# Loading the second half of the last expert's up weight in sixteen pieces of eight rows: a Perceiver layer with 32 experts on one core

## The chip, the cores and the metric

The kernel runs on one core of one Trainium2 chip. The metric is the device time of one execution in microseconds (us). Lower is better. Before the change three runs took 1252.88, 1253.95 and 1255.7 us; the median is 1253.95.

## The reference

The reference is one layer in float32 over 256 tokens of width 512. A cross-attention of the tokens with a context of 25088 rows comes first, then a self-attention with 16 heads, and then a feed-forward part with a shared expert and 32 routed experts. Each part is added to its input. What the change touches is the last of these, cut here to its routed experts:

```python
logits = x @ gate_w                         # 256 x 32
topk_ids = jnp.argmax(logits, axis=-1)      # one expert for each token
scores = jax.nn.sigmoid(jnp.max(logits, axis=-1))[:, None]
xs = x * scores
...                                         # tokens sorted by their expert
g = _grouped_mm(sorted_x, routed_gate_w, tokens_per_expert)   # 512 -> 1024
u = _grouped_mm(sorted_x, routed_up_w, tokens_per_expert)     # 512 -> 1024
d = _grouped_mm(jax.nn.silu(g) * u, routed_down_w, tokens_per_expert)   # 1024 -> 512
...
return (shared_out + routed_out).reshape(b, s, h)
```

Each of the 32 experts has three weights of 2 MB: gate, up and down. All are read once, 201 MB in total.

## The kernel before

**Stages.** The first 780 us are the two attentions, in which TensorE is busy nearly all the time. Then come the experts. The kernel gives each expert 32 places for tokens (`CAP`), and gathers the tokens of four experts at a time into `xg`. For each expert `e` it multiplies `xg` with the gate weight `rg_e` and with the up weight `ru_e` (line 1073; four column blocks fill the 128 rows of a PSUM bank), takes silu of the first and multiplies the two (lines 1091 and 1097), turns the result (line 1107), multiplies it with the down weight `rd_e` (line 1121), copies it out of PSUM (line 101), and adds the rows to their tokens with a product by a 0/1 matrix `selT` (line 1130).

**Weights.** Each weight lies in SBUF as a tile of 128 rows (partitions) of 4096 floats, 16 KB a row. Ten such places (`SLOTS` and `MORE_SLOTS`) take turns. The list `to_come` holds the weights in the order of their use: `rg_1`, `ru_1`, `rd_1`, `rg_2` and so on to `rd_31` (a few of the first weights are loaded apart). When a weight has been used, `done` gives its place to `feed`, which takes the next weight from the list and issues its transfer on the queue of SyncE (SP, line 135). A tiling layer assigns the semaphores and adds the waits. SP handles its instructions in order: an issue that waits holds back all that follow it.

**The last two weights.** `feed` cuts the last up weight `ru_31` into two halves of 2048 columns, and the last down weight `rd_31` into pieces of 2048, 1024 and 1024 columns, so that each product can begin before the whole weight has landed. Columns 0 to 2047 of an up weight are its first two blocks of 128 input features, columns 2048 to 4095 the last two. The product with `ru_31` at line 1073 takes the four blocks in order, with 8 of the 32 matmuls that the trace shows for each; the last 16 need the second half.

**The end.** For the last expert `last_down` (from line 1134) forms the product with `rd_31` in three parts of 256, 128 and 128 columns (line 1147), one for each piece, multiplies each with `selT_last` (line 1159), adds it to the sum `y_sb` (line 1160) and stores the part (line 1161): six stores, five on SP's queue and one on ScalarE's. `keep_clock` (line 107) issues matmuls whose results are not used, at places where TensorE would idle.

Below, `ru_31a` and `ru_31b` are the halves of `ru_31`.

Of the kernel before, what the change touches and what calls it, by code (L numbers as in the profile page):

```python
# [16 lines left out]
P = 128  # L17
# [13 lines left out]
E, I = 32, 1024  # L31
# [17 lines left out]
def perceiver_layer(  # L49
# [23 lines left out]
    nc = tc.nc  # L73
# [54 lines left out]
    def feed(slot):  # L128
        if to_come:
            name, src = to_come.pop(0)  # L130
            w = pool_of[slot].tile([P, 4096], F32, tag=f"w{slot}", name=name)
            ends = {f"ru_{E - 1}": (0, 2048, 4096), f"rd_{E - 1}": (0, 2048, 3072, 4096)}
            ends = ends.get(name, (0, 4096))
            for a, b in zip(ends, ends[1:]):
                nc.sync.dma_start(w[:, a:b], src[:, a:b])
            weights[name] = (w, slot)

    def weight(name, f):
# [2 lines left out]
    def done(name):  # L141
        feed(weights.pop(name)[1])
# [183 lines left out]
    with tc.tile_pool(name="pro", bufs=1) as pro:  # L326
# [76 lines left out]
        r = [[by[:, :, u, g, :] for g in range(2)] for u in range(2)]  # L403
# [53 lines left out]
    for slot in range(3, SLOTS):  # L457
        feed(slot)
# [246 lines left out]
    for slot in range(SLOTS, SLOTS + MORE_SLOTS):  # L705
        pool_of[slot] = late
        feed(slot)
# [675 lines left out]
```

## Time and profile before

The profile is one execution with the hardware profiler on. It took 1255.4 us, of which 1253.5 us are the span that the trace covers.

| | |
|---|---|
| median of three runs | 1253.95 us |
| profiled execution | 1255.4 us, span 1253.5 us |
| mean granted TensorE clock | 0.974 of full speed |
| TensorE (PE) busy | 1146.0 us, 91% of the span |
| VectorE (DVE), ScalarE (ACT), GpSimd (POOL) busy | 579.8, 218.9, 208.4 us |
| read from HBM | 328.82 MB, 263 GB/s over the span |

Times inside the trace count from the span's start. PE stands for TensorE's matmuls, PEld for its loads of weights into the array, SP and SPq for SyncE and its queue. "L135" is line 135 of the kernel. In a line such as "ru<-in_ro_u_dram" the tile left of the arrow is written from the one at its right, and numbers in the names of tiles are left out, so that `ru` stands for all the `ru_e`. "x2" after an issue means that two are shown in one line; its second number then reaches from the start of the first to the end of the last. In square brackets stands how long the engine was idle before, and what released it. "To landing" is the time from an issue to the arrival of its last byte.

### The profile page before, as it was taken

To read this page: it belongs to the slowest core of one execution; us is meant where nothing else is said; L and a number is where in the kernel's file an instruction comes from. 1 tells how busy PE (TensorE), PEld (TensorE's weight loads), DVE (VectorE), ACT (ScalarE), POOL (GpSimd) and SP (SyncE) were. 2 spreads that over 40 slices of the span, in tenths; PEclk is the share of its full clock that TensorE was granted. 3 is DMA by queue.
4 is the path that set the end of the run, shared out by engine and by line. 5 is a ranking of instruction groups with operands and counts; after the bars stand their busy time and mean duration, and the time that the engine had idled before them with its cause. 6 is when DMAs were issued, how large, how long until landed. Compare 5 with 4: busy or idle time off the path is not lost.

```text
span 1253.5 us, 16455 instructions
## 1 busy us (share of the span) xinstructions
PE 1146.0 (91%) x6800; PEld 836.8 (67%) x6800; DVE 579.8 (46%) x1083; ACT 218.9 (17%) x456; POOL 208.4 (17%) x172
## 2 busy tenths in 40 slices
PE   9999999999999999999999999999998777666667
PEld 7888888888888888888888766654544323222223
DVE  3577766786666866668766435421101010110001
ACT  1222221122221222212221223311000000000000
POOL 1234312333223332133322000000000000000000
PEclk9999999999999999999999999899999888898989
DMA  9654444444443444434431391699999999999997
GB/s 384 278 197 166 170 157 151 162 168 168 168 157 146 168 168 168 168 138 165 168 138 65 135 401 36 273 424 428 429 430 429 430 429 428 430 430 429 430 428 307
DMA packets 32765, 330.44 MB, mean 264 GB/s; under 512 B 3760, under 2 KB 4656, under 8 KB 5680
## 3 DMA queue, kind: packets, MB, share of 16 engines
q1 hardware_dynamic: 32400, 329.03, 65.9%
q8 instruction: 55, 0.90, 0.3%
q10 hardware_dynamic: 288, 0.33, 0.1%
q14 instruction: 22, 0.18, 0.0%
HBM read 328.82 MB, written 0.52 MB: 263 GB/s over the span
## 4 chain that ended last, share of the span: by engine, by line
PE 74%; DMA 22%; DVE 2%; issue 1%; ACT 1%; POOL 0%; DVEq 0%; ACTq 0%; SPq 0%
PE sc L483 26%; PE p L299 22%; DMA rd<-in_ro_d_dram 9%; DMA ru<-in_ro_u_dram 6%; DMA rg<-in_ro_g_dram 6%; PE rg L1073 2%; PE acc L1130 2%; PE d L1121 2%; PE ru L1073 2%; PE shg L1180 1%; PE q L753 1%; PE y L821 1%; PE vh L730 1%; PE shu L1180 1%; PE k L753 1%
## 5 line engine op out<-in xcount | busy, mean ns | idle before, releaser
L483 PE MATMUL sc<-aT,ctxT 128*128 128x256 f32 x1568 | 341.1, 379 | 0.0
L483 PEld LDWEIGHTS sc<-aT,ctxT 128*128 128x128 f32 x1568 | 297.8, 190 | 40.7 <-issue 0.2
L299 PE MATMUL p<-diffs,sums 128*128 128x256 f32 x576 | 155.9, 379 | 0.8 <-DVE diffs L285 0.8
L299 PEld LDWEIGHTS p<-diffs,sums 128*128 128x128 f32 x576 | 109.4, 190 | 16.1 <-DVE diffs L285 1.3
L487 ACT COPY st<-sc 128x512 f32<-128x512 f32 x98 | 57.4, 586 | 276.7 <-PE sc L483 276.7
L533 POOL TENSOR_TENSOR ls<-ls,st 128x512 f32<-128x512 f32 x64 | 104.2, 1628 | 3.8
L1121 PE MATMUL d<-rd,actT 128*32 128x512 f32 x496 | 74.0, 709 | 32.5 <-DMA rd<-in_ro_d_dram 25.6
L491 DVE TENSOR_TENSOR mx<-mx,st 128x512 f32<-128x512 f32 x64 | 47.0, 734 | 121.0 <-ACT st L487 120.7
L299 PE MATMUL p<-ctx,st 128*128 128x256 f32 x384 | 98.5, 379 | 0.0
L1073 PE MATMUL ru<-ru,xg 128*32 128x256 f32 x992 | 66.8, 409 | 31.5 <-DMA ru<-in_ro_u_dram 31.5
L1128 DVE TENSOR_SCALAR selT<-keys,slot_key 128x256 f32<-128x256 f32 x31 | 10.9, 354 | 164.6 <-PE acc L1130 164.6
L1097 DVE TENSOR_TENSOR act<-act,ru 128x256 f32<-128x256 f32 x32 | 13.5, 422 | 154.8 <-PE ru L1073 154.8
L299 PEld LDWEIGHTS p<-ctx,st 128*128 128x128 f32 x384 | 73.0, 190 | 9.9
L1130 PE MATMUL acc<-d,selT 128*128 128x512 f32 x124 | 64.2, 642 | 15.1 <-ACT d L101 15.1
L529 ACT ACTIVATE st<-st 128x512 f32<-128x512 f32 x98 | 59.9, 631 | 77.9 <-DVE m L511 73.2
L1073 PEld LDWEIGHTS ru<-ru,xg 128*32 128x32 f32 x992 | 31.7, 116 | 62.2 <-DMA ru<-in_ro_u_dram 39.7
L500 POOL PARTITION_ALL_REDUCE mbc<-mx x17 | 18.8, 1105 | 306.3 <-DVE mx L492 298.5
L526 DVE TENSOR_TENSOR st<-st,mbc 128x512 f32<-128x512 f32 x98 | 62.7, 685 | 0.0
L1073 PE MATMUL rg<-rg,xg 128*32 128x256 f32 x960 | 59.1, 382 | 1.7 <-DMA rg<-in_ro_g_dram 0.7
L1130 PEld LDWEIGHTS acc<-d,selT 128*128 128x128 f32 x124 | 22.1, 198 | 54.8 <-ACT d L101 38.6
L1121 PEld LDWEIGHTS d<-rd,actT 128*32 128x32 f32 x496 | 16.9, 120 | 62.0 <-issue 47.8
L299 PE MATMUL p<-ctx,sums 128*128 128x256 f32 x192 | 57.2, 380 | 0.5 <-DVE sums L280 0.5
(296 smaller groups left out, 1317.2 us busy)
## 6 DMA issues: line engine op xcount, KB each, us to landing
rd<-in_ro_d_dram SPq DMA_DIRECT2D x31, 2048.0 KB, 38.8
ru<-in_ro_u_dram SPq DMA_DIRECT2D x30, 2048.0 KB, 37.5
rg<-in_ro_g_dram SPq DMA_DIRECT2D x30, 2048.0 KB, 38.9
ctxT<-in_cxT_dram SPq DMA_DIRECT2D x49, 1024.0 KB, 4.9
ctx<-in_cx_dram SPq DMA_DIRECT2D x49, 1024.0 KB, 4.9
sh<-in_sh_gu_dram SPq DMA_DIRECT2D x2, 2048.0 KB, 18.6
w_qc_ks<-in_w_qc_ks_dram SPq DMA_DIRECT2D x2, 1024.0 KB, 12.6
w_vc_vs<-in_w_vc_vs_dram SPq DMA_DIRECT2D x2, 1024.0 KB, 15.7
```

What stands on the lines that cost most here:

```text
L299: nc.tensor.matmul(bank[n][:, ts(o, half)], left[:, i, :], right[:, h, :], start=(first and o == 0), stop=(final and (o == 1 or n == 3)),)
L483: nc.tensor.matmul(pm[:, ts(u, N)], cols[b][:, c, ts(2 * h + u, P)], aT[:, c, :], start=(c == 0), stop=(c == KC - 1),)
L487: nc.scalar.copy(st[:, i, :], pm)
L491: nc.vector.tensor_tensor(mx, mx, st[:, i, :], ALU.max)
L526: nc.vector.tensor_tensor(pair, pair, mbc.to_broadcast([P, 2, N]), ALU.subtract)
L529: nc.scalar.activation(st[:, i, :], st[:, i, :], AF.Exp, scale=xscale)
L533: nc.gpsimd.tensor_tensor(ls, ls, st[:, i, :], ALU.add)
L753: nc.tensor.matmul(pm[:, :N], w[:, c, ts(hp, P)], h1T[:, c, :], start=(c == 0), stop=(c == KC - 1),)
L1073: given["up"] = nc.tensor.matmul(pm[ts(q, CAP), : I // 4], xg[:, c, ts(j, CAP)], w[c][:, ts(q, I // 4)], start=(i == 0), stop=(i == KC - 1),)
L1121: nc.tensor.matmul(pd[ts(q, CAP), :], actT[:, k, ts(q, CAP)], wd_e[:, k, q], start=(k == 0), stop=(k == 1),)
L1130: summed = nc.tensor.matmul(accs[t], slT[:, ts(t, P)], d, start=start, stop=stop)
L1180: nc.tensor.matmul(pm[:, :N], w[:, o + c, ts(i % 4, P)], h2T[:, c, :], start=(c == 0), stop=(c == KC - 1),)
```

## The change

The second half of `ru_31` no longer comes in one transfer of 128 rows and 1024 KB. It comes in sixteen transfers of eight rows each, 64 KB a piece, issued on the same queue at the same place, one after the other. The first half and the three pieces of `rd_31` are as before; `rd_31` still follows `ru_31` on the queue.

```diff
@@ -129,10 +129,14 @@
         if to_come:
             name, src = to_come.pop(0)
             w = pool_of[slot].tile([P, 4096], F32, tag=f"w{slot}", name=name)
-            ends = {f"ru_{E - 1}": (0, 2048, 4096), f"rd_{E - 1}": (0, 2048, 3072, 4096)}
+            ends = {f"ru_{E - 1}": (0, 2048), f"rd_{E - 1}": (0, 2048, 3072, 4096)}
             ends = ends.get(name, (0, 4096))
             for a, b in zip(ends, ends[1:]):
                 nc.sync.dma_start(w[:, a:b], src[:, a:b])
+            if name == f"ru_{E - 1}":
+
+                for r in range(0, P, 8):
+                    nc.sync.dma_start(w[r : r + 8, 2048:], src[r : r + 8, 2048:])
             weights[name] = (w, slot)
 
     def weight(name, f):
```

## The prediction

> **What bounds the kernel now.** I read the page first: its slices and its chain.
>
> ```profile
> DMA  9654444444443444434431391699999999999997
> ...
> PE 74%; DMA 22%; DVE 2%; issue 1%; ACT 1%; POOL 0%; DVEq 0%; ACTq 0%; SPq 0%
> ```
>
> The last 15 of 40 slices have the DMA engines full (9) at about 430 GB/s: the stretch in which the experts' weights stream in. Then the chain of waits in order of time, its end:
>
> ```profile
> 1178.27 38.83 DMA rd<-in_ro_d_dram
> 1217.10 0.14 issue
> 1217.23 2.97 PE d L1121 x16
> ```
>
> Up to 1217 us the path is transfers laid end to end; after that TensorE's work for the last three experts runs, close behind the stream. How close, the timeline of the last microseconds tells:
>
> ```profile
> 1240.51 2.13 PE L1073 MATMUL ru<-ru,xg 128*32 128x256 f32 x32
> 1241.57 0.59 PEld L1073 LDWEIGHTS ru<-ru,xg 128*32 128x32 f32 x16 [0.47 <-DMA ru<-in_ro_u_dram]
> ...
> 1245.23 0.38 PEld L1147 LDWEIGHTS d_last<-rd,actT_last 128*32 128x32 f32 x16 [0.43 <-DMA rd<-in_ro_d_dram]
> ```
>
> The second half of ru_31 (the transfer that is changed) and the second piece of rd_31 are each waited for, by 0.47 and 0.43 us. So there is no slack behind them: a later landing is a later end, one for one. An earlier landing can give back at most 0.47 + 0.43 = 0.9 us.
>
> What decides is when SP may issue. The timeline of SP alone:
>
> ```profile
> 1168.44 0.33 SPq L135 DMA_DIRECT2D rg<-in_ro_g_dram  x1
> ...
> 1202.58 5.12 SPq L135 DMA_DIRECT2D ru<-in_ro_u_dram  x2
> 1212.27 10.07 SPq L135 DMA_DIRECT2D rd<-in_ro_d_dram  x3
> ```
>
> The two halves of ru_31 come from one loop, with nothing between them in the code, yet 5.12 us pass from the start of the first issue to the end of the second: the second starts at 1202.58 + 5.12 - 0.33 = 1207.37. The rg issued at 1168.44 needs, by its tile's view,
>
> ```profile
> DMA to landing us min/median/max: 38.9/38.9/38.9
> ```
>
> and lands at 1207.3. It is the eighth transfer before this one. The rule holds at each of the last issues: an issue waits for the landing of the transfer eight before it (38.9 us is also 8 times 2,048 KB at 431 GB/s). The first output store shows it too, in SP's waits and in the view of line 1161:
>
> ```profile
> SPq L1161 <- DMA ru<-in_ro_u_dram: 3.7, 1, 3.7
> ...
> L1161 SPq EVENT_SEMAPHORE  x5: 17/17/32, 1226.9 to 1249.2; - x5
> ```
>
> Its data are ready at 1247, but first it waits until 1226.9 for ru_30, eight transfers earlier and no input of it. So at most eight transfers are in flight, whatever their size. The last five, ru_31 in two and rd_31 in three, take from issue to landing:
>
> ```profile
> DMA to landing us min/median/max: 36.5/36.5/36.5
> ...
> DMA to landing us min/median/max: 34.2/34.2/34.2
> ...
> DMA to landing us min/median/max: 31.7/31.7/31.7
> ...
> DMA to landing us min/median/max: 28.1/28.1/28.1
> ...
> DMA to landing us min/median/max: 24.4/24.4/24.4
> ```
>
> Issued at 1202.6, 1207.4, 1212.3, 1217.1 and 1222.0, they land at 1239.1, 1241.6, 1244.0, 1245.2 and 1246.4.
>
> **The change part by part.** It removes one 1,024 KB transfer and adds sixteen of 64 KB, p0 to p15, ahead of rd_31 on SP's queue. The work of TensorE, VectorE and ScalarE is the same.
>
> *Where the sixteen are issued.* p0 takes the removed transfer's place at 1207.4. By the rule of eight p1 waits for ru_29 (1212.3), p2 rd_29 (1217.1), p3 rg_30 (1222.0), p4 ru_30 (1226.9), p5 rd_30 (1231.8), p6 rg_31 (1236.6), and p7 the first half of ru_31, at 1239.1. When that lands, only p0 to p6 stand behind it (448 KB), where now 3 MB do. These seven hide behind older transfers and cost nothing. p8 to p15 wait for p0 to p7, which land within about 2 us after 1239.1, so SP's own pace sets them.
>
> *SP's pace.* The trace has bursts of issues that wait for nothing, as at the kernel's start:
>
> ```profile
> 2.17 0.43 SPq L156 DMA_DIRECT2D w_kc_qs<-in_w_kc_qs_dram  x1
> 2.65 0.45 SPq L162 DMA_DIRECT2D bias_sb<-in_biases_dram  x1
> 3.13 0.44 SPq L329 DMA_DIRECT2D selT<-in_midT_dram  x1
> ```
>
> One per 0.48 us, and the 26 KB transfer costs no less than the 1 MB ones. Elsewhere a second issue follows after 0.37 (23.04 to 23.41) and a third after 0.54 (to 23.95). No issue of eight rows is in the trace; I take 0.45 with ends of 0.37 and 0.54, since the size does not show.
>
> *The second half of ru_31.* p15 is issued at 1239.1 + 8 x 0.45 = 1242.7. A 1,024 KB load into an idle queue takes 4.8 us (ctx at 112.9 us), of which 2.44 is data at 430 GB/s, so 2.4 is fixed; one 8 KB row on one of 16 engines at 430/16 = 27 GB/s adds 0.3. p15 lands 2.7 later (ends: 1.7, the shortest store of the page, and 3.3, the longest), at 1245.4 instead of 1241.6: +3.8 for the product.
>
> *rd_31.* It is moved from 1212.3 behind p15: 1239.1 + 9 x 0.45 = 1243.15. Its first half needs 4.8 us to 1248.0; its two quarters, 1.22 us of data each, land by 1249.2 and 1250.4, against 1246.4. Since 1239.1 + 4.8 + 2.44 is 1246.4, the delay is nine issues: 9 x 0.45 = 4.05 us (3.3 to 4.9). TensorE reaches d_last at 1244.22 + 3.8 = 1248.0, just as its first piece is there: the two delays lie beside each other, and the larger counts, **+4.1**.
>
> *New waits.* The product now waits for sixteen landings on TensorE's queue; behind it stand actT_last, d_last and part, which need it anyway. A semaphore instruction takes 17 ns in SP's row above, so seven more are 0.1 us, hidden in the idle time before p15 lands. The six output stores now wait for p11 to p15 and rd_31, landed long before their data are ready.
>
> *The clock.* TensorE idles 0.5 us before the second half now, and 4.3 with the change. What such gaps do, two of the earlier ru products show, one beside the other:
>
> ```profile
> 1197.67 3.52 PE L1073 MATMUL ru<-ru,xg 128*32 128x256 f32 x32 [2.91 <-DMA ru<-in_ro_u_dram]
> ...
> 1212.25 1.93 PE L1073 MATMUL ru<-ru,xg 128*32 128x256 f32 x32 [2.91 <-DMA ru<-in_ro_u_dram]
> ```
>
> After the same gap one ran at a granted clock of 0.50 and one at full clock. Half a product at the slow rate loses (3.52 - 1.93)/2 = 0.8. The bounds are 0 (no drop, or hidden behind rd_31) and 3 (all of 1244.2 to 1248.0 slow, at 1.8 times); since the gap is longer than those of 2.9, which already go either way, I take **+0.7**.
>
> [...]
>
> [...]
>
> **Sum.** 4.1 + 0.7 = +4.8 us. The profiled execution took 1255.4 (span 1253.5 and 1.9 around it), so it would take 1260.2. It lies 1.45 above the median of the runs; on the median the forecast is 1253.95 + 4.8 = 1258.75, about **1258.8**. 0.2% is 2.5 us, which is about what a measurement of this kernel can tell from no change.
>
> **The rivals.**
>
> *No bound of eight for such small pieces* (chance 0.10). If all sixteen were queued by 1215 and rd_31 behind them, the stream would never run dry: 1,024 KB more or less on the same engines, no change if the rows spread evenly, at most one more 2.4 us if half the engines carry it all. 1253.9 to 1256.4. Against it: the 4.84 us between issues of every size, the 64 KB-sized store among them.
>
> *Faster through the engines that are ahead* (0.02). DMA engines do not end together: at 1242 to 1246 the busy share is 0.53 and 0.41, so about half of them are done while the others still work. If the eight-row pieces fell on those, the late half would carry 64 KB less each, 2.4 us, and rd_31 would land by 1244. TensorE can use 0.9 of it: 1253.05. It decides only if p7 to p15 are queued before 1239, which the rule of eight forbids.
>
> *Each piece waits for the one before* (0.06). If the program holds the sixteen for overlapping writes of one tile, they go one by one: p1 to p15 at 2.7 + 0.1 each after 1239.3, 42 us, rd_31 after that: near 1253.95 + 40 = 1294. Nothing in the trace has two queued writes to different rows of one tile, so only the code speaks against it: the rows are disjoint.
>
> *The forecast* has 0.82. Within it, the ends 3.3 to 4.9 and 0 to 3 give 1257.2 to 1261.9.
>
> **How the numbers follow.** The range reaches down into the first rival, 1255.4, and up past the likeliest case's end by 0.6 for a p15 that lands as late as 3.3 us, 1262.5. Outside it lie the serial case (0.06), the faster one (0.02), and the part of the first rival under 1255.4 (about 0.06), with some of the forecast's tails. Faster by over 0.2%: 0.02. Within 0.2%: the first rival's 0.10 and 0.02 of the forecast with quick issues. Slower: the rest, 0.86.
>
> **What would show it.** In the changed kernel SP should issue p1 to p6 some 4.9 us apart, p7 to p15 and rd_31 in one burst of 0.4 to 0.5 each after 1239, and rd_31's pieces should take 5 to 7 us to land instead of 24 to 32. The wait for ru at line 1073 should be near 4 us at the last product, DMA share should fall below a third between 1240 and 1244, and everything before 1207 should be as it was. I am wrong if rd_31 is issued before 1239, if the burst is quicker than 0.3 or slower than 0.6 us per piece, or if each piece waits for the one before.

## The result, and the profile after

The changed kernel takes 1263.87 us (median of 6 runs, 1261.89 to 1267.97) against 1252.72 us (6 runs) before: a ratio of 1.0079, interval 1.0063 to 1.0096, or 7.9 to 12 us slower. The forecast was 1258.8 with a range to 1262.5: slower, as said, but by about twice the 4.8 us. The profiled execution took 1264.5 us, with a span of 1262.6, 9.1 more than before.

The page of the changed kernel, its slices of DMA share and its chain by engine:

```profile
DMA  9744444344444445444430573799999999999995
...
PE 73%; DMA 22%; DVE 3%; issue 1%; ACT 1%; POOL 0%; DVEq 0%; ACTq 0%; SPq 0%
```

The stream is full up to the last slice, as before; that one has 5 tenths instead of 7. The shares of the chain hardly move, and TensorE, VectorE and ScalarE do the same work in the same order, so it is the end that has to be read. The chain from ru_31a on, in order of time (start, us, what; pieces under 0.8 us are left out):

```profile
1199.88 37.97 DMA ru<-in_ro_u_dram
1237.87 3.72 DMA ru<-in_ro_u_dram
1241.61 6.03 DMA ru<-in_ro_u_dram
1247.67 1.98 PE ru L1077 x16
1251.42 2.79 PE d_last L1151 x32
1254.21 1.79 PE part L1163 x4
1257.04 0.96 DVE y_sb L1164 x4
```

The first line is ru_31a, the second p7 (issued when ru_31a lands, landed 3.7 us later), the third p15 (issued when p7 lands, landed 6.0 us later). Then TensorE takes over. rd_31 is not on the path at all. SP's timeline of the same kernel:

```profile
1199.88 0.33 SPq L135 DMA_DIRECT2D ru<-in_ro_u_dram  x1
1204.67 37.21 SPq L139 DMA_DIRECT2D ru<-in_ro_u_dram  x16
1242.36 1.79 SPq L135 DMA_DIRECT2D rd<-in_ro_d_dram  x3
```

Inside the 37.21 us the single issues of the trace start at 1204.67 (p0), 1209.52, 1214.41, 1219.31, 1224.20, 1229.10, 1234.98, 1237.87 (p7), 1238.18, 1238.52, 1238.86, 1239.19, 1239.56, 1240.20, 1240.91 and 1241.61 (p15). The rule of eight holds for each: p7 starts 0.02 us after ru_31a has landed at 1237.85, and p13, at 1240.20, 0.02 us after p5 has landed at 1240.18. TensorE's timeline:

```profile
1238.50 1.07 PE L1077 MATMUL ru<-ru,xg 128*32 128x256 f32 x16
1247.67 1.93 PE L1077 MATMUL ru<-ru,xg 128*32 128x256 f32 x16 [8.10 <-DMA ru<-in_ro_u_dram]
...
1251.42 2.79 PE L1151 MATMUL d_last<-rd,actT_last 128*32 128x256 f32 x32 [0.52 <-DVE actT_last L99]
```

The second half of the last up product waits 8.1 us, and then the same 16 matmuls take 1.93 us where the first 16 took 1.07; d_last takes 2.79 against 1.66 before. The same end in the timeline of the kernel before, with the last additions to the sum:

```profile
1244.22 1.66 PE L1147 MATMUL d_last<-rd,actT_last 128*32 128x256 f32 x32 [0.52 <-DVE actT_last L99]
...
1247.99 0.96 DVE L1160 TENSOR_TENSOR y_sb<-y_sb,part 128x128 f32<-128x128 f32 x4 [0.57 <-PE part L1159]
```

Last, stretches of 2 us (busy time of PE, PEld, DVE, ACT and POOL; then the granted clock, the DMA share and GB/s), first before, then after:

```profile
1240.00:1242.00 2.00, 2.00 (x27) 0.88 (x29) 0.00 (x0) 0.00 (x0) 0.00 (x0) 1.00 0.90 363
```

```profile
1240.00:1242.00 2.00, 0.00 (x0) 0.00 (x0) 0.00 (x0) 0.00 (x0) 0.00 (x0) 1.00 0.49 90
1242.00:1244.00 2.00, 0.00 (x0) 0.00 (x0) 0.00 (x0) 0.00 (x0) 0.00 (x0) 0.50 0.78 123
1244.00:1246.00 2.00, 0.00 (x0) 0.00 (x0) 0.00 (x0) 0.00 (x0) 0.00 (x0) 0.50 0.96 143
...
1252.00:1254.00 2.00, 2.00 (x32) 1.04 (x24) 0.00 (x0) 0.37 (x1) 0.00 (x0) 0.50 0.00 0
```

Two things stand here that the forecast did not have. The DMA engines are busy for half of their time (0.49) and move 90 GB/s: 11 GB/s for each busy one (90 / (0.49 x 16)), where a full queue moves 430 / 16 = 27. And the granted clock is 0.50 from 1242 to 1254 at least.

**Where the time went.** From the landing of ru_31a to the start of the last additions the kernel took 1247.99 - 1239.11 = 8.9 us before and 1257.04 - 1237.87 = 19.2 after. Of the 10.3 us between them, 7.4 lie before the last landing of ru_31 (2.4 us after ru_31a before the change, 9.8 after it) and 2.9 behind it (6.5 against 9.4 us, the halved clock). Another 1.5 us lie ahead of that landing: ru_31a itself took 38.0 us from issue to landing, where it took 36.5 before, and rg_31 ahead of it 40.0 instead of 39.0. From the issue of ru_31a on that is 11.8 us in all. The spans differ by 9.1, because in the second profile ru_31a happened to be issued 2.7 us earlier (1199.88 against 1202.58), ahead of anything that the change adds.

### The profile page after: what moved, and what is told of

Read it like the earlier page. It is cut to its first block, busy times and chain, and to the rows that moved or that the text cites. A ratio compares the mean times of both kernels' runs of the same rounds, so it can differ in the third digit from the quotient of the medians.

```text
span 1262.6 us, 16474 instructions
## 1 busy us (share of the span) xinstructions
PE 1143.3 (91%) x6800; PEld 835.9 (66%) x6800; DVE 581.1 (46%) x1083; ACT 218.8 (17%) x456; POOL 208.4 (17%) x172
## 4 chain that ended last, share of the span: by engine, by line
PE 73%; DMA 22%; DVE 3%; issue 1%; ACT 1%; POOL 0%; DVEq 0%; ACTq 0%; SPq 0%
PE sc L487 26%; PE p L303 22%; DMA ru<-in_ro_u_dram 10%; DMA rg<-in_ro_g_dram 6%; DMA rd<-in_ro_d_dram 6%; PE rg L1077 2%; PE ru L1077 2%; PE d L1125 2%; PE acc L1134 2%; PE shg L1184 1%; PE q L757 1%; PE acc L1196 1%; PE y L825 1%; PE vh L734 1%; PE shu L1184 1%; PE k L757 1%
## 5 line engine op out<-in xcount | busy, mean ns | idle before, releaser
L1077 PE MATMUL ru<-ru,xg 128*32 128x256 f32 x992 | 66.7, 409 | 41.1 <-DMA ru<-in_ro_u_dram 41.1
L1134 PEld LDWEIGHTS acc<-d,selT 128*128 128x128 f32 x124 | 22.1, 198 | 55.3 <-ACT d L101 39.1
```

What stands on the lines that cost most here:

```text
L1077: given["up"] = nc.tensor.matmul(pm[ts(q, CAP), : I // 4], xg[:, c, ts(j, CAP)], w[c][:, ts(q, I // 4)], start=(i == 0), stop=(i == KC - 1),)
L1134: summed = nc.tensor.matmul(accs[t], slT[:, ts(t, P)], d, start=start, stop=stop)
```

## The experiments

**Theories.** T1, the prediction's: the price is that of SP's issues, which begin when ru_31a lands, and of an empty queue behind them. T2: a transfer of few neighbouring rows is itself slow. T3: the halved clock is what doubles the loss. The edits replace the loop of the changed kernel at lines 138 and 139; the two with fillers (matmuls whose results are not used) keep it and add matmuls. Times are medians in us, beside the kernel before on the same chip.

| pieces of the second half | this | before | ratio [interval] |
|---|---|---|---|
| 16 of 128 columns, all rows | 1258.89 | 1253.79 | 1.0044 [1.0030, 1.0057] |
| 8 of 256 columns, all rows | 1256.24 | 1254.19 | 1.0015 [1.0004, 1.0027] |
| 16 of eight rows, four apart on both sides | 1262.36 | 1253.79 | 1.0067 [1.0045, 1.0089] |
| the same, four apart in HBM alone | 1265.25 | 1253.42 | 1.0091 [1.0063, 1.0119] |
| the same, four apart in SBUF alone | 1263.38 | 1253.42 | 1.0076 [1.0057, 1.0095] |
| 2 of 64 neighbouring rows | 1264.07 | 1253.79 | 1.0079 [1.0052, 1.0106] |
| 2 of every other row | 1253.89 | 1253.42 | 1.0003 [0.9990, 1.0016] |
| neighbours in SBUF, every other in HBM | 1263.71 | 1254.19 | 1.0070 [1.0043, 1.0098] |
| every other in SBUF, neighbours in HBM | 1253.63 | 1254.19 | 0.9998 [0.9986, 1.0011] |
| 8 of 16 neighbouring rows | 1259.54 | 1254.19 | 1.0031 [1.0018, 1.0044] |
| sixteen of eight rows, 11 filler rounds | 1262.06 | 1253.79 | 1.0063 [1.0043, 1.0083] |
| sixteen of eight rows, 22 filler rounds | 1264.53 | 1253.42 | 1.0084 [1.0062, 1.0105] |

**As many issues, but all rows (T1 alone).** Sixteen pieces of 128 columns, each over all 128 rows:

```diff
-for r in range(0, P, 8):
-    nc.sync.dma_start(w[r : r + 8, 2048:], src[r : r + 8, 2048:])
+for c in range(2048, 4096, 128):
+    nc.sync.dma_start(w[:, c : c + 128], src[:, c : c + 128])
```

> Sixteen transfers again at the same place, but each of all 128 rows and 128 columns (512 bytes a row) instead of eight rows and 2048 columns. The number of issues, the eight in flight and the 64 KB stay. Theory A (neighbouring rows share a way): all ways are used, the data of a piece take about 0.15 to 0.3 us, SP's pace of 0.34 us decides, the last piece lands some 5 us after the first half and the time is near 1257. Theory B (a fixed completion cost for each small transfer): the pieces still land 0.7 us apart, 9 to 10 us in all, near 1263. What is left above the time before is, by theory A, the price of the sixteen issues behind a limit of eight in flight.

It lost 5.1 us by the medians. SP's timeline and the chain of this kernel:

```profile
1204.44 35.89 SPq L139 DMA_DIRECT2D ru<-in_ro_u_dram  x16
1240.43 1.32 SPq L135 DMA_DIRECT2D rd<-in_ro_d_dram  x3
```

```profile
1240.85 6.45 DMA rd<-in_ro_d_dram
```

ru_31a landed at 1236.19, and rd_31 was issued 1240.43 - 1236.19 = 4.24 us later (forecast: 4.05), at one issue per 0.475 us. rd_31 is on the path (the chain's line is its second piece), and its last piece landed 12.4 us after ru_31a where it was 7.3 before: +5.0, for a forecast of 4.1. This is the mechanism that was forecast, at nearly its price. The clock adds to it: from the landing of rd_31's second piece to the last additions it took 3.8 us instead of 2.8, with a granted clock of 0.53 from 1246 to 1248. ru_31a took 36.5 us, as before. Eight rows cost nearly as much again on top (ratio 1.0079 against 1.0044).

**Half as many issues.** The same with `range(2048, 4096, 256)` and pieces of 256 columns.

> Eight transfers of 128 rows and 256 columns instead of sixteen of 128 columns (which cost 5 to 5.5 us). By the limit of eight in flight seven of the eight are issued before the first half of ru_31 has landed and wait in the queue; only the eighth and rd_31 come after it. The prediction's sum, number of issues after that landing times SP's pace, gives one issue, 0.4 to 0.5 us, more for rd_31; the product waits for the eighth, some 2 us after it is issued, as before the change. If the limit of eight is what the sixteen pay for, the time is within 2 us of the kernel before; if small transfers cost by their number, it is half of 5.3, 1256 to 1257.

It lost 2.05 us, which lies on the border of the two cases that were expected, so the time does not decide between them; the trace says more. Only the last piece waits for ru_31a, and rd_31 is issued 0.45 us after ru_31a has landed; still its last piece lands 9.4 us after ru_31a, 2.1 later than before. The queue runs nearly empty in any case (240 GB/s from 1236 to 1242, where it was 403 before), and then rd_31's first piece needs 5.7 us from issue to landing. So the nine issues are not the whole of T1's price: a start into a drained queue is part of it.

**Rows four apart.** Eight rows a piece still, but spread over a block of 32:

```diff
+for r in range(16):
+    rows = slice(r // 4 * 32 + r % 4, r // 4 * 32 + 32, 4)
+    nc.sync.dma_start(w[rows, 2048:], src[rows, 2048:])
```

> The same sixteen transfers of eight rows of 8 KB, but the eight rows of one lie four rows apart (0, 4, ... 28), in HBM and in SBUF. In the changed kernel half the DMA engines are busy from 1240 to 1242 us and move only 90 GB/s, 11 GB/s each instead of 27, so a piece takes its engines about 0.72 us. Theory A (neighbouring rows share a way, into SBUF or out of HBM): a row needs about 0.31 us again, the pieces land at SP's pace of 0.34 us, the last one lands about 5 us after the first half of ru_31 instead of 9.8, the wait at the last up product falls from 8.1 us to 3 or 4, and the time to some 1257. Theory B (every small transfer costs its engines a fixed 0.4 us for the completion, whatever its rows): nothing changes, 9.8 us and 1263. Theory C (the eight engines in use are slow because only eight are): nothing changes either.

By its time it can't be told from the change, but the time goes elsewhere. The pieces of the burst now land 2.4 to 2.5 us after their issue, close to the forecast's 2.7, with the last at 3.9; but SP needs 0.67 us for each instead of 0.31 to 0.37, so rd_31 is issued 6.1 us after ru_31a and p15 lands 9.3 us after it (9.8 in the changed kernel). Two kernels followed that spread the rows on one side only. In the one the source rows are `src[rows]` and the target `w[8 * r : 8 * r + 8]`, in the other the reverse; the half weight lies in HBM in the order that this needs.

> With rows four apart on both sides a row took about 0.31 us again, but SP needed 0.67 us per issue. Here only the HBM side is four apart (rows 0, 4, ... 28 of a block; the host stores the rows of this half weight accordingly, so the result is the same), and a piece is written into eight neighbouring rows of SBUF. Theory A1 (the shared way is the one into SBUF): rows are slow, 0.7 us each while only pieces move, and half the DMA engines move about 90 GB/s; last piece 9 to 10 us after the first half of ru_31, time 1262 to 1264. Theory A2 (the shared way is out of HBM): rows take 0.31 us, 2.5 us from issue to landing.

> The other half: a piece is read from eight neighbouring rows of HBM, as in the change, and written into rows four apart in SBUF. Theory A1 (way into SBUF): rows take 0.31 us, a piece lands 2.5 us after its issue, and if SP's issue is quick (0.3 us) the last piece lands some 6 us after the first half of ru_31 and the time is near 1258; if the SBUF stride is what makes SP slow (0.67 us), some 8 us and 1261. Theory A2 (out of HBM): rows take 0.7 us, time 1262 to 1264.

By time they can't be told apart (1.0063 to 1.0119 and 1.0057 to 1.0095). The trace tells what the two sides do. The tile's view of SP's issues (ns, shortest, median and longest), first of the changed kernel, then with the rows apart in SBUF alone:

```profile
L139 SPq DMA_DIRECT2D ru<-in_ro_u_dram x16: 272/272/347, 1204.7 to 1241.6; - x16
```

```profile
L140 SPq DMA_DIRECT2D ru<-in_ro_u_dram x16: 623/624/802, 1206.0 to 1243.1; - x16
```

The chains show ru_31a and the last piece, first with the rows apart in HBM alone, then in SBUF alone:

```profile
1204.07 38.19 DMA ru<-in_ro_u_dram
...
1245.34 4.20 DMA ru<-in_ro_u_dram
```

```profile
1201.24 36.52 DMA ru<-in_ro_u_dram
...
1243.13 3.72 DMA ru<-in_ro_u_dram
```

Spread in SBUF, an issue costs 0.62 us instead of 0.27, and its pieces are quick (2.4 to 2.6 us after issue but for the last, 3.7). Spread in HBM alone, an issue costs 0.27 and the pieces are slower (3.1 to 4.2 us), and so are the big transfers beside them: ru_31a takes 38.2 us, against 36.5 before and with the rows apart in SBUF. So what slows the big transfers is the SBUF side, and there the gain is paid back by SP.

A rival is that a transfer of eight rows is slow because it keeps only half of the DMA engines busy. It does seem to keep half of them: the DMA share was 0.49 while such pieces were alone, and in the trace the semaphore of each piece is updated once 0.5 us after the issue and eight times as the piece lands, that of a transfer of 128 rows sixteen times. But the pieces with the rows apart in SBUF show the same nine updates and are quick (2.4 to 2.6 us for all but the last).

**Few and large: halves of 64 rows.** To have fewer rows without many issues, the second half in two transfers: rows 0 to 63 and 64 to 127, or every other row.

```diff
+for r in range(0, P, 64):
+    nc.sync.dma_start(w[r : r + 64, 2048:], src[r : r + 64, 2048:])
```

```diff
+for r in range(2):
+    nc.sync.dma_start(w[r::2, 2048:], src[r::2, 2048:])
```

> The second half of ru_31 in two transfers of 64 rows (0 to 63 and 64 to 127) instead of sixteen of eight. Only one issue more than before the change, so the limit of eight in flight hardly counts. Theory A in the form that the way into SBUF is shared (64 neighbouring rows have half of the ways): each of the two takes 2.4 us of data instead of 1.2, the half lands about 2.4 us later than before, unless engines that are ahead overlap the two; the time is 1253 to 1256. Theory A in the form that neighbouring rows collide in HBM only when eight are read at once, and theory B: as before the change within 1 us.

> Two transfers of 64 rows again, but the even rows and the odd rows instead of the first 64 and the last 64. With the first and the last 64 the DMA engines were full from 1236 to 1248 us and moved only 225 to 238 GB/s, and the time was 1264. Theory A1: even rows reach all the ways into SBUF that the 128 rows reach, the stream runs at about 430 GB/s to its end and the time is within 1.5 us of the kernel before the change. Theory D (a transfer of fewer than 128 rows is slow for another reason, such as fewer rows for each engine): slow again, about 1264.

The first is as slow as the change (1.0079), with one issue more than before instead of fifteen; the second can't be told from before. To see which side, one kernel has neighbours in SBUF and every other row in HBM (`w[64 * r : 64 * r + 64]`, `src[r::2]`), one the reverse.

> Two transfers of 64 rows, which need one issue more than the kernel before the change, so that SP's pace plays no part. They are written into the first 64 and the last 64 rows of SBUF, but read from every other row of HBM (the host stores the rows of this half weight accordingly). Both sides neighbouring took 1264 with packets of 8 KB at 0.55 to 0.6 us; both sides every other row took 1254 with 0.31. Theory A1 (the shared way is into SBUF): packets at 0.5 to 0.6 us, about 230 GB/s from 1236 on with the DMA engines full, time 1262 to 1265. Theory A2 (out of HBM): 0.31 us, about 430 GB/s, time 1253 to 1255.

> The reverse: read from the first 64 and the last 64 rows of HBM, written into every other row of SBUF. Theory A1: 0.31 us a packet, 1253 to 1255. Theory A2: 0.5 to 0.6 us, 1262 to 1265.

Again SBUF alone decides: 1.0070 against 0.9998. The windows of the last microseconds with a full queue: before; then both sides neighbours; neighbours in SBUF alone; neighbours in HBM alone:

```profile
1236.00:1242.00 6.00, 5.50 (x63) 2.51 (x65) 0.69 (x1) 0.97 (x2) 0.00 (x0) 1.00 0.97 403
```

```profile
1236.00:1242.00 6.00, 3.33 (x36) 1.27 (x34) 0.69 (x1) 0.84 (x2) 0.00 (x0) 1.00 0.99 229
```

```profile
1236.00:1242.00 6.00, 3.01 (x35) 1.13 (x33) 0.69 (x1) 0.97 (x2) 0.00 (x0) 1.00 1.00 231
```

```profile
1234.00:1238.00 4.00, 3.69 (x36) 1.61 (x36) 0.69 (x1) 0.84 (x2) 0.00 (x0) 1.00 1.00 421
```

The engines are busy all the time (0.97 to 1.00), and yet they move half as much where 64 neighbouring rows of SBUF are written. The DMA records say how: a row of 8 KB takes 0.31 us before and 0.55 in the kernel with neighbours in SBUF alone (medians from 1230 to 1240 and from 1232 to 1243). It is not these two transfers alone that are slow. The tile view of the gate weight that is in flight beside them, rg_31, all 128 rows of it, with neighbours on both sides and with neighbours in HBM alone (39.0 before, too):

```profile
DMA to landing us min/median/max: 41.2/41.2/41.2
```

```profile
DMA to landing us min/median/max: 39.0/39.0/39.0
```

**A dose between.** Eight pieces of 16 neighbouring rows (`range(0, P, 16)`).

> Eight transfers of sixteen neighbouring rows instead of sixteen of eight: all sixteen DMA engines may take part, one row each, and SP has half the issues, so the limit of eight costs little (see the eight transfers of 256 columns). Theory A1 (neighbouring rows of SBUF share a way): still slow, about 100 to 150 GB/s while the pieces move, 7 to 10 us for the 1024 KB instead of 2.4, time 1260 to 1264. Theory C (the eight-row pieces were slow because a transfer of eight rows uses eight engines only): about 400 GB/s, time within 2 us of the kernel before.

It lost 5.35 us by the medians (3.9 by the ratio), between the eight pieces of all rows (2.05) and the change. The window with pieces in flight:

```profile
1236.00:1242.00 6.00, 4.07 (x52) 2.03 (x52) 0.00 (x0) 0.58 (x2) 0.00 (x0) 1.00 0.64 191
```

ru_31a took 39.1 us instead of 36.5, and the last piece 4.2 us to land, more than with all rows (2.6 in the eight pieces of 256 columns) and less than eight rows (6.0). TensorE's timeline has a clue on the clock:

```profile
1244.73 1.07 PE L1077 MATMUL ru<-ru,xg 128*32 128x256 f32 x16 [2.88 <-DMA ru<-in_ro_u_dram]
...
1247.37 2.79 PE L1151 MATMUL d_last<-rd,actT_last 128*32 128x256 f32 x32 [0.52 <-DVE actT_last L99]
```

The product behind a gap of 2.88 us runs at full clock, and d_last, 1.6 us after it, at half.

**The clock.** Fillers (`keep_clock`) between the two halves of the last up product, in the changed kernel:

```diff
-product(pu, wu_e)
+product(pu, wu_e, between=lambda: keep_clock(tr_bank(f"hold_{name}"), between, act[:, :P], act))
...
```

First with 11 rounds, then with 22, for the last expert alone.

> The changed kernel with 11 more rounds of keep_clock between the two halves of the last up product, about 6 us of matmuls whose results are not used, in a wait of 8.1 us. In the changed kernel the granted clock is 0.50 from 1242 to 1254, and from the landing of the last piece to the end of the last product takes 9.4 us where it took 6.4 before. If that is the clock: the last 16 matmuls of the product take 1.07 us instead of 1.93 and d_last 1.66 instead of 2.79, the time falls by 2 to 3 us to about 1261, and the wait for the pieces itself is unchanged, 8 us less the fillers. If it is not: no change.

> As the run with 11 more rounds of keep_clock, with 22. The 11 rounds were over 4 us before the last piece landed, and the clock fell all the same, to 0.50 from 1246 on, so that run told nothing on the clock. 22 rounds should last until the landing, 8 to 10 us. If the clock is the second term: TensorE keeps its full clock to the end, the last 16 matmuls of the product take 1.07 us, d_last about 1.7, and the time falls by 2 to 3 us, to about 1261, less what the fillers overshoot. If not: no change.

TensorE's timeline with 11 rounds:

```profile
1238.53 5.02 PE L107 MATMUL hold<-act 128*128 128x256 f32 x22
1247.57 1.94 PE L1077 MATMUL ru<-ru,xg 128*32 128x256 f32 x16 [4.02 <-DMA ru<-in_ro_u_dram]
```

The 11 rounds ended at 1243.5, 4 us before the data came, and the clock was halved all the same (0.50 to 0.51 from 1246 to 1256): this run decides nothing. With 22 rounds it stayed full (1.00 from 1232 to 1256):

```profile
1251.96 1.07 PE L1077 MATMUL ru<-ru,xg 128*32 128x256 f32 x16
...
1254.60 1.51 PE L1154 MATMUL d_last<-rd,actT_last 128*32 128x256 f32 x32 [0.52 <-DVE actT_last L99]
```

The product is back at 1.07 and d_last at 1.51, and from the last landing to the last additions it took 7.4 us instead of 9.4, although the fillers ran 1.1 us past that landing. The time did not fall, though (1264.53): in this profile the last piece landed 10.6 us after ru_31a instead of 9.8. So that the clock costs 2.9 us is read from the durations in the traces; no run shows it in the time. T3 is no more than that: 2.9 of the 11.8 us, and not the half of the loss.

## Why the prediction was wrong, point by point

*Where the issues stand: right.* At most eight are in flight, p0 to p6 are issued ahead and p7 at the landing of ru_31a. But "These seven hide behind older transfers and cost nothing" is wrong by 1.5 us: they slowed ru_31a, which took 38.0 us (37.5 and 37.6 in the two kernels with fillers) and 36.5 wherever the pieces had all rows or rows apart in SBUF. The term was put at nothing because a piece was taken to move like other traffic. The rival without the bound of eight and the one with a gain both needed the pieces to be queued before that landing, and p8 was issued 0.3 us after it. (The store that the prediction set against the first, as one of 64 KB, moves 128.) The rival of pieces one by one is out too: they landed 0.3 to 1.0 us apart.

*SP's pace: taken from other shapes.* An issue of eight neighbouring rows takes 0.27 us, less than the lower end of 0.37 to 0.54; p8 to p12 follow 0.31 to 0.37 apart. But p13 to p15 and rd_31 come 0.64 to 0.75 apart, because each waits for a piece eight before it that has not landed. The step that p0 to p7 "land within about 2 us", so that SP's own pace sets the rest, failed there: p7 landed 3.7 us after ru_31a. By accident the nine issues still came to 4.5 us (forecast 4.05).

*p15's flight: the step that failed.* A row of 8 KB at 27 GB/s was to add 0.3 us, so that p15 lands 2.7 us after its issue, with an upper end of 3.3. It took 6.0. The rate per engine was taken from full transfers and carried to eight neighbouring rows, which the trace of before could not show. Between 1240 and 1242 a row of 8 KB took 0.72 us in the DMA records (0.31 before), so the pieces came in 0.7 us apart and p15 stood behind them. Half of the engines at 27 GB/s would have moved 215 GB/s; they moved 90. The runs show that transfers into neighbouring rows of SBUF are slow (229 and 231 GB/s with halves of 64 neighbouring rows, 421 with neighbours in HBM alone), and slow what is in flight with them (ru_31a took 38.0 us beside the pieces instead of 36.5). This made the product's delay 7.4 us where 3.8 was forecast. The upper bound came from lines of the page (stores) that say nothing of a loaded queue, and so the range missed.

*Which delay counts: the other one.* rd_31 was said to be the larger. It is later too (its first piece takes 7.4 us, not 4.8), but lands at 1249.8, before d_last can start at 1251.4, and the other two (1251.0 and 1252.2) land ahead of their use: it lies beside the product's delay. Where the pieces have all rows (16 of 128 columns), rd_31 does set the end, and there the sum of 4.8 met a loss of 5.1.

*The clock: mis-sized.* +0.7 was taken from bounds of 0 and 3; the traces show 2.9. The gap was 8.1 us, not 4.3.

*The signs.* The wait of the last product was to be near 4 us and was 8.1; rd_31's pieces were to take 5 to 7 us and took 7.4 to 8.4. The DMA share between 1240 and 1244 was to fall below a third. It was 0.49 and 0.78, though only 90 and 123 GB/s moved: busy engines are not a full rate.

So of 11.8 us from ru_31a's issue to the last additions, the forecast had 4.8. Missing are 1.5 for the slower ru_31a, 7.4 - 4.1 = 3.3 from slow rows behind it and 2.9 - 0.7 = 2.2 from the clock, which fell for longer.

**Open.** For halves of 64 rows the SBUF side alone decides. For the burst of eight-row pieces after ru_31a it does not explain all: with neighbours on both sides (the change and the two kernels with fillers) the last piece landed 9.8 to 10.8 us after ru_31a, in the change 0.6 to 1.0 us apart for most, but 7.3 us after it with the rows apart in HBM alone, at 0.3 to 0.5 apart for most. The times of the two can't be told apart, and no run tells why. Ahead of the burst both slow ru_31a alike (38.0 and 38.2 us). And no run here shows what inside the chip the rows share.

## What to carry to other kernels

A transfer's price depends on which rows of SBUF it writes: cut a tile by columns, or into even and odd rows, and not into blocks of neighbouring rows, which here, at 64 rows, nearly halved the rate of everything in flight (231 GB/s against 421). Count transfers against the number that may be in flight: past it, each small piece takes the place of a large one, and the queue runs dry (here past eight: with sixteen pieces of 128 columns 137 GB/s from 1236 to 1242, where it was 403 before). A rate taken from full transfers is no bound for a shape that the trace does not show (27 GB/s for an engine there, 11 here); a range should then reach to the slowest rate per engine that the case allows.

## What the runs showed of the hardware

- An issue on SP takes 0.27 us for eight neighbouring rows, 0.33 to 0.43 for pieces of `ru_31` of all 128 rows, and 0.62 for eight rows four apart in SBUF.
- Halving a transfer by every other row costs nothing that can be measured (0.9986 to 1.0016 over the two kernels); halving it into neighbouring rows of SBUF costs 9 to 10 us.
- The clock can fall some time after a gap: with pieces of 16 rows the product behind a gap of 2.88 us ran at full clock (1.07 us), and d_last, 1.6 us after it, at half.
- Transfers into neighbouring rows of SBUF slow the transfers of all 128 rows that are in flight with them: 36.5 us from issue to landing became 37.5 to 38.2 beside pieces of eight rows, 39.1 beside 16, and 41.1 beside 64 on both sides. Beside 64, rg_31 took 41.2 and 41.4 instead of 39.0.
